# A macaron layer on one core: the latent masks and rows of constants move from the front of the program into the plan of its first half

## The chip, the cores and the metric

The kernel runs on one core of a Trainium2 chip. The metric is the device time of one execution in microseconds (us); lower is better. The core has five engines that run beside each other and wait for each other through semaphores: TensorE (PE, with its weight loads shown as PEld), VectorE (DVE), ScalarE (ACT), GpSimd (POOL) and SyncE (SP), which issues DMA transfers here. Each engine works through its own instructions strictly in the order in which the program lists them.

## The reference

The input x is 8 sequences of 512 tokens with 128 channels. The computation is two half-weighted blocks around a latent attention:

```python
x = x + 0.5 * ffn(layernorm(x))       # DEPTH = 2 layers of local attention and a gated MLP
x = x + attn(layernorm(x))            # causal attention, 16 heads of 8 channels
x = x + 0.5 * ffn(layernorm(x))       # the same weights again
```

A layer of `ffn` projects to q, k and v for 8 heads of 64 channels, normalises q and k, turns them by a rotary table, attends within windows of 64 tokens and the window before, and adds a product with `wo`; then a layernorm, a product with `w1`, `a * gelu(g)` and a product with `w2`. In `attn` the scores are masked so that a query sees only itself and the tokens before it, and the softmax runs over those.

## The kernel before, in words

Sequences b = 0 to 7 are cut into four blocks of 128 tokens. The program has three parts, one after the other: the first `ffn` with the beginning of the latent attention (`ffn("f0", last=False)`), the latent attention itself (`latent_attention`), and the second `ffn` (`ffn("f1", last=True)`).

In front of them stand loads and constants. Constants are made on POOL, in this order: the identity (by a helper in masks.py) and its 16-bit copy (L288), two band masks for the local attention (L294 to L306), and then what the latent attention needs: three masks `rows_of`, `causal` and `causal_t` of 128 x 512 in 16 bits, each by one memset (L317) and four `affine_select`, one for each quadrant of 32 partitions (L325), and `rows_sb`, two rows of constants (L332). `fill_rows` copies such a row by DMA into the tiles of the latent heads (L335); `maximum_products` and `sum_products` give the masks to TensorE (L1288, L1346 and their like).

Each `ffn` is written as steps, and a planner, `Plan`, puts them in order. A step has a kind, an engine, a cost in us that is written beside it, a rank, what it reads and writes, and the buffers that it takes. The rank is 100 times the number of the token block that the step belongs to, plus an entry of the table PLACE by kind. `Plan.run` deals out one step at a time: it looks at the steps in its window (for the `ffn` the 110 of lowest rank, `AHEAD`), works out from the written costs when each could start, takes the engine of the one that can start first, and on this engine the step of lowest rank that can start by then. It then traces the step, and binds each instruction behind the one before it on the same engine. So one more step on an engine changes the time at which the planner believes that engine to be free, and with it the order in which later steps are dealt, on the other engines too.

The constants in front are no steps: the planner begins with every engine free at time 0 and knows nothing of them. But they stand on POOL before POOL's first steps.

The steps that matter around the change, by lines:

- a layernorm: statistics on DVE (L484 to L486), logarithm and exponential on ACT (L467, L468) for the inverse root, a Newton step of four small instructions on POOL (L471 to L474), the result on DVE (L492)
- transposes of it on PE (L504), copied by ACT and DVE into `hT` (L528, L520); the first column of the lower half of `hT` is zeroed on POOL (L524)
- products with `wqkv` (L542); q and k are squared on ACT (L568) and multiplied by the rotary tables on DVE (L552, L555; the tables are made at L346 and L350), added on POOL (L576); the sums of squares on DVE (L600, L603), their root on ACT and its Newton step on POOL, and the scaling of k on POOL (L612)
- transposes of q and k (L504, copied at L642), scores (L665, L675), their maximum (L684, L685), the exponential on ACT (L692), the division by the sum on POOL (L700; its reciprocal on DVE, L716), transposes, the product with v (L758) and with `wo` (L782)
- products of weights for the latent attention, made once by `latent_weights` (L984 to L1004, rank of block 4 or 5 less 400)
- the beginning of the latent attention, at the end of the first plan (`latent_begins`): row fills by SP (kind "lo") and masked products of q and k for the maxima (kind "lm")

Of the kernel before, what the change touches and what calls it, by code (L numbers as in the profile page):

```python
# [10 lines left out]
BF16 = mybir.dt.bfloat16  # L11
AF = mybir.ActivationFunctionType
ALU = mybir.AluOpType
# [3 lines left out]
P = 128  # L17
MASKED = -1.0e30
# [15 lines left out]
}  # L34


# [152 lines left out]
def kernel(  # L189
# [21 lines left out]
    nc = tc.nc  # L211
# [80 lines left out]
    for first in (True, False):  # L292
        band = const.tile([P, P], BF16, name=f"band{int(first)}")
        nc.gpsimd.memset(band, 0.0)  # L294
        for half in (0, WIN):
            rows = band[half : half + WIN]
# [14 lines left out]
    def quadrant(g):  # L311
        return slice(32 * g, 32 * g + 32)

    masks = {}
    for name in ("rows_of", "causal", "causal_t"):
        masks[name] = const.tile([P, 4, P], BF16, name=name)
        nc.gpsimd.memset(masks[name], 0.0)  # L317
    for g in range(4):
        for name, pattern, sign, op, fill in (
            ("rows_of", [[-32, 4], [1, P]], -1, ALU.not_equal, 1.0),  # L320
            ("causal", [[32, 4], [-1, P]], 1, ALU.is_ge, MASKED),
            ("causal_t", [[-32, 4], [1, P]], -1, ALU.is_ge, MASKED),
        ):
            rows = masks[name][quadrant(g)]
            nc.gpsimd.affine_select(  # L325
                out=rows, in_=rows, pattern=pattern, compare_op=op, fill=fill, base=0,
                channel_multiplier=sign,
            )

    rows_sb = const.tile([4, 2, P], F32, name="rows_sb")  # L330
    for k in range(2):
        nc.gpsimd.memset(rows_sb[:, k], float(k))  # L332

    def fill_rows(dst, k):
        nc.sync.dma_start(  # L335
            out=dst[MD::32].rearrange("p j (n t) -> p (j n) t", t=P),
            in_=rows_sb[:, k].unsqueeze(1).to_broadcast([4, 4 * NB, P]),
        )
# [69 lines left out]
    def ffn(tagname, last):  # L408
        plan = Plan(tc, nc)

        def step(kind, engine, cost, at, *args, **kw):
            return plan.step(kind, engine, cost, 100 * at + PLACE[kind], *args, **kw)
# [514 lines left out]
        def first_loads():  # L927

            tables_u = Slot(r_u)
            size = 4 * NB * DH  # L930

            def rotary():
                return flat(tables_u.tile)[:, :size].rearrange(
                    "p (f n d) -> p f n d", f=4, n=NB
                )

            def scales():
                return flat(tables_u.tile)[:, size : size + 2 * L * DH].rearrange(
                    "p (s l d) -> p s l d", s=2, l=L
                )  # L940

            for t, scale in enumerate((q_scale, k_scale)):
                load_step(
                    0, lambda t=t, scale=scale: nc.sync.dma_start(
                        out=scales()[:, t].rearrange("p l d -> p (l d)"),
                        in_=scale.rearrange("l d -> (l d)").partition_broadcast(P),
                    ), [tables_u], [tables_u],
                )
            load_step(0, lambda: nc.sync.dma_start(out=rotary(), in_=rot), [tables_u], [tables_u])
            for l in range(L):  # L950
                for t in range(2):
                    step(
                        "tb", DVE, 1.2, 2 * l,
                        lambda l=l, t=t: rotary_table(l, t, rotary(), scales()),
                        [tables_u], [("tab", l, t)], [tables_u],
                    )
            load_step(0, lambda: nc.sync.dma_start(out=cols_sb, in_=cols), [("W", 0)])
            for what in load_layer(0):
                load_step(1, what, [("W", 0)])
            for b in range(1, B):  # L960
                load_step(NB * b, lambda b=b: load_tokens(b), [("X", b)])
            load_step(
                NB * 3, lambda: nc.sync.dma_start(out=wqkv_sb[1], in_=wqkv[1]), [("W", 1)]
            )
            for what in load_layer(1):
                load_step(NB * 4, what, [("W", 1)])
            latent_weights()

        def latent_weights():

            room, at = Slot(r_u), [0]

            def piece(rows, n):
                at[0] += n
                return lambda a=at[0]: flat(room.tile)[:rows, a - n : a]

            w = {}
            for name, src in (
                ("dq", w_dq), ("uq", w_uq), ("uq_t", w_uq_t), ("dkv", w_dkv), ("uk", w_uk),
                ("uv", w_uv), ("o_t", w_o_t),  # L980
            ):
                w[name] = piece(*src.shape)
                load_step(
                    4, lambda name=name, src=src: nc.sync.dma_start(out=w[name](), in_=src),  # L984
                    [("lw", name)], [room],
                )
            w["a"], w["keff"], w["veff"] = piece(QL, KVL), piece(KVL, C), piece(KVL, C)
            for n, name in enumerate(("full_q", "full_k", "full_v")):
                w[name] = lambda n=n: full[n]
            for lhsT, rhs, name in (  # L990
                ("uq", "uk", "a"), ("a", "dq", "keff"), ("uv", "o_t", "veff"),
                ("dq", "uq_t", "full_q"), ("dkv", "keff", "full_k"), ("dkv", "veff", "full_v"),
            ):
                ps = Slot(mm)

                def product(lhsT=lhsT, rhs=rhs, name=name, ps=ps):
                    rows, n = w[name]().shape
                    nc.tensor.matmul(
                        ps[:rows, :n], lhsT=w[lhsT](), rhs=w[rhs](), start=True, stop=True
                    )  # L1000

                def keep(name=name, ps=ps):
                    rows, n = w[name]().shape
                    nc.vector.tensor_copy(w[name](), ps[:rows, :n])  # L1004

                step("lw", PE, 0.3, 5, product, [("lw", lhsT), ("lw", rhs)], [ps], [ps, room], 0.1)
                step("lw", DVE, 0.25, 5, keep, [ps], [("lw", name)], [ps, room], 0.1)

        def latent_begins():
# [4 lines left out]
            for b in range(2):  # L1014
                q, kk, v = Slot(r_kT), Slot(r_V), Slot(r_V2)
                for name, t in (("q", q), ("k", kk), ("v", v)):
                    head_slots[name, b] = t
                    step(
                        "lz", POOL, 1.95, k, lambda t=t: nc.gpsimd.memset(t.tile, 0.0),
                        [], [t], [t], 0.0, [done[L - 1, B - 2 + b, NB - 1], done[L - 1, B - 1, 0]],  # L1020
                    )
                step("lo", SP, 0.55, k, lambda kk=kk: fill_rows(kk.tile, 1), [kk], [kk], [kk], 1.8)
                step(
                    "lz", POOL, 0.3, k,
                    lambda b=b: nc.gpsimd.memset(heads("v", b)[:, :, :, MD : MD + 1], 1.0),
                    [v], [v], [v],
                )
# [49 lines left out]
            for b, held in [(0, held) for held in MAXIMA] + [(1, held) for held in MAXIMA[:LEAD]]:  # L1077
                q, kk = head_slots["q", b], head_slots["k", b]
                m = maxima_of(b)
                for half in (0, 1):  # L1080
                    banks = [Slot(mm), Slot(mm)]
                    units = [
                        (2 * half + n, lambda n=n, banks=banks: banks[n].tile) for n in range(2)
                    ]
                    step(
                        "lm", PE, 1.3, k,
                        lambda b=b, held=held, units=units: by_turns(
                            [maximum_products(b, held, g, bank) for g, bank in units]
                        ),
                        [(q, "d"), (kk, "d")], banks, [q, kk] + banks, 0.1,  # L1090
                    )
                    for (g, bank), t in zip(units, banks):
                        step(
                            "lr", DVE, 0.63, k,
                            lambda m=m, held=held, g=g, bank=bank: maximum(m, held, g, bank()),
                            [t], [("max", b, g)], [t], 0.0,
                        )
# [521 lines left out]
```

## Time and profile before

| | us |
|---|---|
| median of 3 runs | 1879.91 |
| the runs | 1884.78, 1879.69, 1879.91 |
| profiled execution | 1883.39 |
| its span | 1881.6 |
| PE busy | 1757.7 |
| ACT busy | 1389.6 |
| DVE busy | 1373.7 |
| POOL busy | 990.1 |
| granted TensorE clock, mean | 0.98 of full |

Times in the profile are counted from the start of the span. A row of the timeline gives start, duration, engine, line of the kernel, operation, the tiles written and read, and in brackets how long the engine stood idle before it and what it waited for; rows that follow each other with the same form are merged with their count (x4). Durations overlap a little on one engine, because an instruction starts before the one ahead of it has quite ended. A row of the windows gives a stretch of time, its length, the busy time of each engine with the number of instructions, the granted clock, the busy share of the DMA engines and what they moved in GB/s. A suffix of _f on a tile's name means that it belongs to one of the two `ffn`.

### The profile page before, as it was taken

Reading aid. Unit: us, or ns where it says so; the run is one execution under the profiler, and the core shown is the slowest. Engines: PE = TensorE matmul, PEld = TensorE weight load, DVE = VectorE, ACT = ScalarE, POOL = GpSimd, SP = SyncE. Lnnn points to the kernel's source line nnn. Section 1 sums busy time; section 2 is a strip of 40 time slices with the busy share of each in tenths; the row PEclk is TensorE's granted clock in tenths of the full one; section 3 lists DMA queues with packets and bytes.
Section 4 is the critical chain, followed back from the end, with each engine's and each line's share of the span. In section 5 each row is a group of like instructions: output and inputs, shape, how many; then the busy total and the mean of one; then the engine's idle time right before and its main releaser. Section 6 shows DMA issues by size and latency. Waiting matters only on the chain.

```text
span 1881.6 us, 50927 instructions
## 1 busy us (share of the span) xinstructions
PE 1757.7 (93%) x19860; PEld 1179.0 (63%) x19860; DVE 1373.7 (73%) x2884; ACT 1389.6 (74%) x3911; POOL 990.1 (53%) x1685
## 2 busy tenths in 40 slices
PE   4899999999999989899999998989999999999998
PEld 2556666666666666467777764666666666666665
DVE  6888887777777867666766746878877777777764
ACT  2888878888888777236666666878888788778885
POOL 5776766666666665100000005867766666666651
PEclk9999999999999999769999999999999999999999
DMA  3111111111111111000000000111111111111110
GB/s 105 45 38 30 29 24 24 24 27 24 24 24 30 24 24 22 26 10 19 15 16 15 15 3 18 27 23 25 26 25 27 24 25 29 30 29 35 29 33 24
DMA packets 51968, 50.04 MB, mean 27 GB/s; under 512 B 22758, under 2 KB 34704, under 8 KB 51728
## 3 DMA queue, kind: packets, MB, share of 16 engines
q1 hardware_dynamic: 51584, 46.00, 10.5%
q8 instruction: 158, 2.59, 0.6%
q14 instruction: 82, 0.67, 0.1%
q10 hardware_dynamic: 144, 0.79, 0.1%
HBM read 6.30 MB, written 2.10 MB: 4 GB/s over the span
## 4 chain that ended last, share of the span: by engine, by line
PE 56%; DVE 18%; ACT 14%; POOL 6%; issue 4%; DMA 1%; SPq 1%; ACTq 0%; DVEq 0%; POOLq 0%
PE mm_f L542 9%; PE mm_f L504 8%; ACT pr_f L692 5%; PE mm_f L849 5%; PE st L1355 4%; PE mm_f L891 4%; PE mm_f L758 4%; PE mm_f L782 3%; PE lo L1372 3%; PE sc L1297 3%; DVE c_f L552 3%; DVE s_f L555 3%; PE sc_f L675 3%; ACT sq_f L568 2%; PE mm_f L1297 2%
## 5 line engine op out<-in xcount | busy, mean ns | idle before, releaser
L692 ACT ACTIVATE pr_f<-sc_f,nm_f,q_f 128x128 f32<-128x128 f32 x1024 | 460.3, 475 | 5.5 <-DVE nm_f L685 5.1
L542 PE MATMUL mm_f<-wqkv,hT_f 128*128 128x512 f32 x768 | 391.3, 613 | 30.4 <-DVE s_f L555 14.0
L576 POOL TENSOR_TENSOR qk_f<-c_f,s_f 128x512 f32<-128x512 f32 x256 | 325.0, 1274 | 115.1 <-DVE s_f L555 112.8
L700 POOL TENSOR_TENSOR pr_f<-pr_f,rso_f 128x512 f32<-128x512 f32 x256 | 266.0, 1040 | 220.8 <-DVE rso_f L716 180.7
L552 DVE TENSOR_TENSOR c_f<-mm_f,tab 128x512 f32<-128x512 f32 x256 | 175.3, 685 | 79.0 <-PE mm_f L542 34.6
L692 ACT ACTIVATION_READ_ACCUMULATOR pr_f<-sc_f,nm_f,q_f 128x1 f32 x1024 | 226.4, 221 | 0.0
L568 ACT ACTIVATE sq_f<-mm_f 128x512 f32<-128x512 f32 x256 | 153.1, 608 | 87.4 <-DVE s_f L555 61.4
L1366 ACT ACTIVATE pl<-st 128x512 f32<-128x512 f32 x280 | 152.8, 597 | 73.9 <-PE st L1355 59.8
L849 PE MATMUL mm_f<-fT_f,w 128*128 128x512 f32 (+1 forms) x384 | 190.5, 611 | 8.9 <-ACT ge_f L855 7.0
L504 PEld LDWEIGHTS mm_f<-ident,qk_f 128*128 128x128 f32 x1024 | 114.7, 141 | 128.9 <-POOL qk_f L612 52.1
L504 PE MATMUL mm_f<-ident,qk_f 128*128 128x128 f32 x1024 | 160.0, 280 | 31.8 <-POOL qk_f L612 12.8
L542 PEld LDWEIGHTS mm_f<-wqkv,hT_f 128*128 128x128 f32 x768 | 125.0, 192 | 99.1 <-issue 42.0
L684 DVE TENSOR_REDUCE nm_f<-sc_f 128x8 f32<-128x1024 f32 x128 | 155.3, 1214 | 42.6 <-PE sc_f L675 42.5
L758 PEld LDWEIGHTS mm_f<-pT_f,V_f 128*64 128x64 f32 (+1 forms) x4096 | 147.4, 136 | 60.2 <-issue 13.1
L758 PE MATMUL mm_f<-pT_f,V_f 128*64 128x64 f32 (+1 forms) x4096 | 179.8, 230 | 0.7 <-ACT pT_f L738 0.7
L555 DVE TENSOR_TENSOR s_f<-mm_f,tab 128x512 f32<-128x512 f32 x256 | 174.0, 680 | 0.0
L1387 POOL TENSOR_TENSOR X<-X,lon 128x128 f32<-128x128 f32 x26 | 11.9, 456 | 306.2 <-DVE lon L1381 306.2
L504 PE MATMUL mm_f<-ident,pr_f 128*128 128x128 f32 x1024 | 155.9, 280 | 11.5 <-DVE u_f L880 3.0
L504 PEld LDWEIGHTS mm_f<-ident,pr_f 128*128 128x128 f32 x1024 | 116.3, 142 | 74.1 <-POOL pr_f L700 33.0
L600 DVE TENSOR_REDUCE rn_f<-sq_f 128x16 f32<-128x1024 f32 x128 | 153.7, 1201 | 7.5 <-ACT sq_f L568 7.5
L782 PEld LDWEIGHTS mm_f<-wo,oT_f 128*128 128x128 f32 x1024 | 127.7, 191 | 43.0 <-ACT oT_f L771 18.1
L782 PE MATMUL mm_f<-wo,oT_f 128*128 128x128 f32 x1024 | 140.7, 280 | 3.2 <-ACT oT_f L771 2.9
(166 smaller groups left out, 3865.2 us busy)
## 6 DMA issues: line engine op xcount, KB each, us to landing
V_f<-V_f SPq DMA_DIRECT2D x224, 128.0 KB
hs_f<-Y SPq DMA_DIRECT2D x32, 112.0 KB
X<-in_x_dram SPq DMA_DIRECT2D x8, 256.0 KB
out_dram<-hs_f SPq DMA_DIRECT2D x8, 256.0 KB
Y<-fl SPq DMA_DIRECT2D x32, 32.0 KB
kT_f<-fl SPq DMA_DIRECT2D x32, 32.0 KB
V_f<-fl SPq DMA_DIRECT2D x32, 32.0 KB
wqkv<-in_wqkv_dram ACTq DMA_DIRECT2D x1, 768.0 KB
```

Source lines behind the costliest of these rows:

```text
L504: nc.tensor.transpose(dst[:, i * P : (i + 1) * P], src(i), ident)
L542: nc.tensor.matmul(ps.tile, lhsT=hT[:, i * P : (i + 1) * P], rhs=wqkv_sb[l][:, at * INNER : (at + 1) * INNER], start=True, stop=True,)
L552: nc.vector.tensor_mul(c1.tile, psv, tabs[l][:, 2 * s, i].unsqueeze(1).to_broadcast([P, H, DH]))
L555: nc.vector.tensor_mul(s1.tile.rearrange("p h (t d) -> p h t d", t=2), psv.rearrange("p h (t d) -> p h t d", t=2)[:, :, ::-1], tabs[l][:, ...
L568: lambda s=s, ps=ps: nc.scalar.activation(sq[:, s], ps.tile, AF.Square),
L576: lambda s=s, c1=c1, s1=s1: nc.gpsimd.tensor_add(qk[:, s].rearrange("p (h d) -> p h d", d=DH), c1.tile, s1.tile),
L684: nc.vector.tensor_reduce(nm.tile, sv, AX.X, ALU.max, negate=True)
L692: nc.scalar.activation(pr[:, h], sv[:, h % 2, h // 2], AF.Exp, bias=nm[:, h % 2, h // 2 : h // 2 + 1], scale=q8[:, h : h + 1], accum_out=s ...
L700: nc.gpsimd.tensor_mul(pr[:, heads], pr[:, heads], inv[:, heads].unsqueeze(2).to_broadcast([P, H // 2, P]),)
L758: nc.tensor.matmul(o[r * DH : (r + 1) * DH, u * P + w * WIN : u * P + (w + 1) * WIN], lhsT=(V2, V)[w][keys, i, h * DH : (h + 1) * DH], rhs ...
L782: nc.tensor.matmul(pw[:, :C], lhsT=oT[:, pr], rhs=wo_sb[l][:, pr], start=(pr == 0), stop=(pr == INNER // P - 1),)
L849: nc.tensor.matmul(ps[: hsz[c], :], lhsT=w1_sb[l][:, at + c * P : at + c * P + hsz[c]], rhs=fT.tile, start=True, stop=True,)
```

## The change

The masks and the rows of constants get their tiles in front as before, but the instructions that fill them become 17 steps of kind "lb" on POOL in the first plan: three memsets, twelve selects and two small memsets. Each has a written cost of 0.65 us and a rank of 500, that of token block 5. The four selects of a mask now follow its memset; before, the selects went around the three masks. The row fills of `latent_begins` and the products for its maxima name "masks" among what they read, so that the planner puts them behind the 17 steps. The rows of the second row fill ("l4") stay as they are.

```diff
-    "lw": -400, "tb": -450, "fi": 990, "fo": 1230,
+    "lw": -400, "lb": 0, "tb": -450, "fi": 990, "fo": 1230,
...
-    masks = {}
-    for name in ("rows_of", "causal", "causal_t"):
-        masks[name] = const.tile([P, 4, P], BF16, name=name)
-        nc.gpsimd.memset(masks[name], 0.0)
-    for g in range(4):
-        for name, pattern, sign, op, fill in (
...
-            rows = masks[name][quadrant(g)]
-            nc.gpsimd.affine_select(
-                out=rows, in_=rows, pattern=pattern, compare_op=op, fill=fill, base=0,
-                channel_multiplier=sign,
-            )
+    MASKS = (
+        ("rows_of", [[-32, 4], [1, P]], -1, ALU.not_equal, 1.0),
+        ("causal", [[32, 4], [-1, P]], 1, ALU.is_ge, MASKED),
+        ("causal_t", [[-32, 4], [1, P]], -1, ALU.is_ge, MASKED),
+    )
+    masks = {name: const.tile([P, 4, P], BF16, name=name) for name, *_ in MASKS}
 
     rows_sb = const.tile([4, 2, P], F32, name="rows_sb")
-    for k in range(2):
-        nc.gpsimd.memset(rows_sb[:, k], float(k))
+
+    def mask_parts():
+
+        for name, pattern, sign, op, fill in MASKS:
+            yield lambda name=name: nc.gpsimd.memset(masks[name], 0.0)
+            for g in range(4):
+                rows = masks[name][quadrant(g)]
+                yield lambda rows=rows, pattern=pattern, sign=sign, op=op, fill=fill: (
+                    nc.gpsimd.affine_select(
...
+        for k in range(2):
+            yield lambda k=k: nc.gpsimd.memset(rows_sb[:, k], float(k))
...
             latent_weights()
+            for what in mask_parts():
+                step("lb", POOL, 0.65, 5, what, [], ["masks"])
...
-                step("lo", SP, 0.55, k, lambda kk=kk: fill_rows(kk.tile, 1), [kk], [kk], [kk], 1.8)
+                step(
+                    "lo", SP, 0.55, k, lambda kk=kk: fill_rows(kk.tile, 1), [kk, "masks"], [kk],
+                    [kk], 1.8,
+                )
...
-                        [(q, "d"), (kk, "d")], banks, [q, kk] + banks, 0.1,
+                        [(q, "d"), (kk, "d"), "masks"], banks, [q, kk] + banks, 0.1,
```

More of the change, by code (lines that the diff above doesn't have):

```diff
@@ L312, in quadrant @@
         return slice(32 * g, 32 * g + 32)
-    masks = {}
-    for name in ("rows_of", "causal", "causal_t"):
-        masks[name] = const.tile([P, 4, P], BF16, name=name)
-        nc.gpsimd.memset(masks[name], 0.0)
-    for g in range(4):
-        for name, pattern, sign, op, fill in (
[L320 to L323, printed above, removed]
-            rows = masks[name][quadrant(g)]
-            nc.gpsimd.affine_select(
-                out=rows, in_=rows, pattern=pattern, compare_op=op, fill=fill, base=0,
-                channel_multiplier=sign,
-            )
-    rows_sb = const.tile([4, 2, P], F32, name="rows_sb")
-    for k in range(2):
-        nc.gpsimd.memset(rows_sb[:, k], float(k))
+    MASKS = (
[4 more added lines that the diff above has]
+    masks = {name: const.tile([P, 4, P], BF16, name=name) for name, *_ in MASKS}
+    rows_sb = const.tile([4, 2, P], F32, name="rows_sb")
+    def mask_parts():
[5 more added lines that the diff above has]
+                    nc.gpsimd.affine_select(
+                        out=rows, in_=rows, pattern=pattern, compare_op=op, fill=fill, base=0,
+                        channel_multiplier=sign,
+                    )
+                )
+        for k in range(2):
+            yield lambda k=k: nc.gpsimd.memset(rows_sb[:, k], float(k))
     def fill_rows(dst, k):
@@ L1021, in latent_begins @@
                     )
-                step("lo", SP, 0.55, k, lambda kk=kk: fill_rows(kk.tile, 1), [kk], [kk], [kk], 1.8)
+                step(
+                    "lo", SP, 0.55, k, lambda kk=kk: fill_rows(kk.tile, 1), [kk, "masks"], [kk],
+                    [kk], 1.8,
+                )
                 step(
```

## The prediction

> **What bounds the kernel now.** First the page's lines by engine and by slice: TensorE is busy for 93% of the span, GpSimd (POOL) for 53%. The chain of waits gives POOL 6% of the span, and TensorE is almost empty in the first slice. So I read the timeline of the first 20 us, which is where the removed instructions stand.
>
> ```profile
> span 1881.6 us, 50927 instructions
> ## 1 busy us (share of the span) xinstructions
> PE 1757.7 (93%) x19860; PEld 1179.0 (63%) x19860; DVE 1373.7 (73%) x2884; ACT 1389.6 (74%) x3911; POOL 990.1 (53%) x1685
> ```
>
> ```profile
> 4.00 0.65 POOL L301 TENSOR_SCALAR_AFFINE_SELECT band<-band 64x128 bf16<-64x128 bf16 x2
> 4.71 0.53 POOL L317 MEMSET rows_of<- 128x512 bf16 x1
> ...
> 6.22 0.63 POOL L325 TENSOR_SCALAR_AFFINE_SELECT rows_of<-rows_of 32x512 bf16<-32x512 bf16 x1
> ...
> 8.33 0.21 ACT L468 ACTIVATE ns_f<-ns_f 128x4 f32<-128x4 f32 x1
> ...
> 13.67 0.34 POOL L332 MEMSET rows_sb<- 4x128 f32 x2
> 14.06 0.14 POOL L524 MEMSET hT_f<- 64x1 f32 x2
> 14.28 0.20 POOL L471 TENSOR_TENSOR nt_f<-ns_f 128x4 f32<-128x4 f32 x1
> ...
> 15.12 0.20 POOL L474 TENSOR_TENSOR ns_f<-ns_f,nt_f 128x4 f32<-128x4 f32 x1
> 15.36 1.12 DVE L492 TENSOR_SCALAR Y<-X,mv_f,ns_f 128x128 f32<-128x128 f32 x4 [7.30 <-POOL ns_f L474]
> ...
> 15.76 1.24 PE L504 MATMUL mm_f<-ident,Y 128*128 128x128 f32 x4 [15.76 <-DVE Y L492]
> ```
>
> The first column is the start, the second the duration. The first layernorm has left ScalarE at 8.54 (8.33 + 0.21), but its Newton step on POOL starts at 14.28, behind the masks; VectorE waits 7.30 us for it, and TensorE starts at 15.76. The chain runs through L317 and L325 here.
>
> Then the stage into which the change moves the masks: POOL's timeline and the windows (busy time of PE, PEld, DVE, ACT, POOL).
>
> ```profile
> 73.35 1.26 POOL L576 TENSOR_TENSOR qk_f<-c_f,s_f 128x512 f32<-128x512 f32 x1
> 78.71 1.27 POOL L576 TENSOR_TENSOR qk_f<-c_f,s_f 128x512 f32<-128x512 f32 x1 [4.10 <-DVE s_f L555]
> 79.94 1.04 POOL L700 TENSOR_TENSOR pr_f<-pr_f,rso_f 128x512 f32<-128x512 f32 x1
> 82.29 1.27 POOL L576 TENSOR_TENSOR qk_f<-c_f,s_f 128x512 f32<-128x512 f32 x1 [1.30 <-DVE s_f L555]
> ```
>
> ```profile
> 79.00:112.00 33.00, 30.42 (x338) 19.80 (x337) 26.96 (x54) 26.56 (x88) 26.45 (x49) 1.00 0.18 42
> 112.00:150.00 38.00, 34.18 (x334) 22.22 (x335) 29.52 (x68) 31.78 (x98) 25.70 (x40) 1.00 0.12 25
> 150.00:250.00 100.00, 98.45 (x1040) 67.12 (x1039) 85.78 (x191) 84.18 (x255) 68.75 (x120) 1.00 0.13 31
> ```
>
> POOL has one hole of 4.10 us, then is busy for 80% of 79 to 112 (26.45 of 33). TensorE stands idle for 8% there (2.58 us), 10% in the next stretch, and 1.6% in the one after.
>
> **Removed in front.** Three memsets, twelve selects and two small memsets hold POOL from 4.71 to 14.01: 9.30 us (memsets 0.47 apart, selects 0.60 apart). Without them POOL ends its constants at 4.65 and does the two hT_f memsets, and the Newton step can start 0.07 after ScalarE (27.40 + 0.21 to 27.68 in the second norm): at 8.61 instead of 14.28, that is **5.67 us** earlier, not 9.30; what is late next is ScalarE's root. The order of each engine stays the same up to the masks' new place, so the whole ramp moves together unless a load holds it. The loads bear it, by the trace's records of DMA packets: the rotary table's (4096 bytes) have all landed at 10.04, and its first reader (L346, 16.39 now) would want it at 10.72; the first wqkv has landed before 6; and X's second batch, landed by 14.82, is wanted at 25.24 - 5.67 = 19.6. I take -5.67.
>
> **Added in the plan.** The same 17 instructions, now in 17 steps; none issues a DMA. In the order of the changed program they stand on POOL from place 92 to 117 of 1690, between the L576 that is at 73.35 now and the stage at some 95 us. The first seven (two memsets, five selects: 2 x 0.47 + 5 x 0.60 = 3.94) come before the L700 of 79.94 and so fall into the 4.10 us hole: nothing. If that cover were gone they would cost up to their 3.94. The other ten (9.30 - 3.94 = 5.36) stand between the steps that run from 79.94 to 95.04. Queued behind them are the divide of the probabilities (L700), the k side's rotary sum (L576) and the Newton step of the q and k norms; TensorE waits for these to transpose. From below: POOL's waits up to 95 (1.30 + 0.46 + 0.51 = 2.27) and 1.33 more by 97.65 take them in, and the chain between 79 and 112 passes through PE, DVE and ACT and no POOL row: 0 us. From above: all 5.36 arrive at TensorE. I take what is left when the waits before 95.04 are used up, 5.36 - 2.27 = **+3.1 us**, because from 98.6 to 111.5 POOL has no wait in which to catch up.
>
> **Reordered.** The planner sees POOL taken and deals the other steps differently: POOL, ScalarE and VectorE come back to the old order at what is now 246.9, 249.9 and 250.4 us. The work is the same; only TensorE's idle time can change. Bounds: it can give back no more than the 2.58 us idle of 79 to 112 where the masks lie, and it can keep TensorE idle at the 10% of 112 to 150 through the 100 us after it as well (rival 2). I put the rest at zero: work of the same size in a similar mix.
>
> **New waits.** The row fills (SP, first at 733.6) and the maxima's products (L1288, first at 771.5) wait for masks that are finished some 600 us before: nothing on SP or PE. The latent half and the second plan keep their order.
>
> **Clock.** Granted clock is 0.84 in 28 to 60, and the trace has half-clock stretches of 6.83 and 3.41 us there; at half clock the weight loads of L542 are 0.85 apart (19.42, 20.28), later 0.43 (22.77, 23.20). If one such 3.41 us stretch comes or goes when the ramp moves, that is 1.7 us either way; I put zero. [...]
>
> **Sum.** -5.67 + 3.1 + 0 = -2.6 us. The profiled execution took 1883.39 (span 1881.6 and 1.8 around it), so 1880.8 by its own measure; it stands 3.5 above the median of the runs, 1879.91, to which I apply the same difference: **1877.3 us**, or -0.14%. A change of 0.3% (5.6 us) is about what a measurement of this kernel can tell from none; its own runs lie between 1879.69 and 1884.78.
>
> **Rivals.**
> 1. *All hidden.* POOL's waits swallow the ten instructions and the reordering gives back some of TensorE's 2.58 us: -5.67 to -8.25, 1871.7 to 1874.2, say 1873. For it: no POOL row on the chain of that stage. Against: POOL's unbroken 13 us from 98.6.
> 2. *Ragged until the orders meet (slower).* The late k side leaves scores and probabilities late, and TensorE idles in 150 to 250 as in 112 to 150: 10.1% - 1.55% = 8.5 us more, on top of all 5.36: -5.67 + 13.9 = +8.2, 1888. It decides once the added idle time exceeds 5.67 us. For it: the order is changed for 170 us, and TensorE has only 1.55 us of idle time in the last 100 to lose. Against: rings of two to five buffers, and ACT and DVE at 84 and 86%, so not full.
> 3. *The front does not pay.* Something else holds the ramp (a load, the clock), the saving is gone and the 3.1 us stay: 1883. Against: the landings above.
>
> **How the numbers follow.** Forecast 0.50 (its own range, from all hidden to 5.36 us: 1874.2 to 1879.6); rival 1 0.27; rival 2 0.17; rival 3 0.06. Rival 1 lies beyond -0.3% (below 1874.3): faster 0.27. Rival 2 lies mostly above 1885.6: slower 0.16, its remaining 0.01 with the forecast and rival 3 within 0.3%: 0.57. The range leaves a little on each side: from 1871.5 (rival 1 with the idle time given back) to 1886 (most of the way to rival 2).
>
> **What would show it.** In the changed profile: the first Newton step at 8.6 and TensorE's first matmul at 10.1; selects of about 0.63 us in a row in POOL's former hole, at some 69 to 73; the latent half's first products (771.5 now) earlier by the net change, 2.6, since nothing after 250 us is reordered. If they are earlier by 5.7 or more, rival 1; if later, rival 2. I am wrong if TensorE's idle time between the hole and the meeting of the orders grows by more than 5.36 us or not at all.

## The result and the profile after

The changed kernel takes 1877.92 us in the median of 21 runs, the kernel before 1881.18 in 21 runs beside them: 3.3 us less. The ratio is 0.9981 with a 95% interval of 0.9973 to 0.9990, so between 1.9 and 5.1 us of gain, and within the 0.3% that the prediction gave as its bound. It had said -2.6 us. The profiled execution took 1879.79 us.

The page of the changed kernel gives the span and the busy times, with hardly a difference from before: the work is the same.

```profile
span 1878.0 us, 50920 instructions
## 1 busy us (share of the span) xinstructions
PE 1759.4 (94%) x19860; PEld 1178.8 (63%) x19860; DVE 1373.3 (73%) x2884; ACT 1384.8 (74%) x3911; POOL 988.8 (53%) x1685
```

The timeline of its start shows the front (lines after the change are four to nine higher in number: L475 was L471, L496 was L492, L508 was L504, L330 was L325).

```profile
3.98 0.62 POOL L301 TENSOR_SCALAR_AFFINE_SELECT band<-band 64x128 bf16<-64x128 bf16 x2
4.56 0.13 POOL L528 MEMSET hT_f<- 64x1 f32 x2
...
8.23 0.20 ACT L472 ACTIVATE ns_f<-ns_f 128x4 f32<-128x4 f32 x1
...
8.59 0.20 POOL L475 TENSOR_TENSOR nt_f<-ns_f 128x4 f32<-128x4 f32 x1 [3.90 <-ACT ns_f L472]
...
9.66 1.11 DVE L496 TENSOR_SCALAR Y<-X,mv_f,ns_f 128x128 f32<-128x128 f32 x4 [1.70 <-POOL ns_f L478]
...
10.06 1.25 PE L508 MATMUL mm_f<-ident,Y 128*128 128x128 f32 x4 [10.06 <-DVE Y L496]
```

POOL now waits 3.90 us for ScalarE, where before ScalarE's result lay waiting for POOL, and TensorE begins at 10.06, 5.7 us earlier than before. POOL's timeline in the former hole and behind it:

```profile
67.35 1.27 POOL L580 TENSOR_TENSOR qk_f<-c_f,s_f 128x512 f32<-128x512 f32 x1
68.57 0.53 POOL L326 MEMSET rows_of<- 128x512 bf16 x1
69.17 2.66 POOL L330 TENSOR_SCALAR_AFFINE_SELECT rows_of<-rows_of 32x512 bf16<-32x512 bf16 x4
71.89 0.52 POOL L326 MEMSET causal<- 128x512 bf16 x1
72.48 0.63 POOL L330 TENSOR_SCALAR_AFFINE_SELECT causal<-causal 32x512 bf16<-32x512 bf16 x1
73.47 1.04 POOL L704 TENSOR_TENSOR pr_f<-pr_f,rso_f 128x512 f32<-128x512 f32 x1 [0.36 <-DVE rso_f L720]
74.58 1.30 POOL L330 TENSOR_SCALAR_AFFINE_SELECT causal<-causal 32x512 bf16<-32x512 bf16 x2
...
81.09 2.66 POOL L330 TENSOR_SCALAR_AFFINE_SELECT causal_t<-causal_t 32x512 bf16<-32x512 bf16 x4
83.83 1.04 POOL L704 TENSOR_TENSOR pr_f<-pr_f,rso_f 128x512 f32<-128x512 f32 x1
```

The first seven stand in the hole, which ends with a wait of 0.36 us, and the other ten lie between the steps behind it. The windows of the changed kernel over the stretch that answers to 79 to 250 of before:

```profile
73.00:107.00 34.00, 31.64 (x342) 21.18 (x343) 26.00 (x55) 26.34 (x87) 30.37 (x52) 0.95 0.15 33
107.00:145.00 38.00, 34.84 (x375) 23.07 (x372) 31.18 (x72) 31.43 (x100) 27.37 (x49) 1.00 0.14 33
145.00:246.00 101.00, 97.48 (x999) 65.44 (x998) 82.00 (x191) 83.47 (x255) 68.56 (x120) 1.00 0.13 29
```

POOL is now busy for 30.37 of 34 us where the masks are. TensorE's idle time is not worse there (2.36 us, against 2.58 in 33 us before); over all three rows it is 9.04 us in 173, against 7.95 in the 171 of the three rows before. But in the first row the granted clock is 0.95: the trace has a stretch of 3.41 us at half clock from 74.1.

**How the traces are compared from here on.** One kernel's times scatter by some 2 us from run to run, as much as the effect. So the lead is also read from the traces: the start of each ScalarE instruction less the start of the same instruction in one and the same trace of the kernel before (its second one, run e7_before_again), and of these the median over ten microseconds. Negative is earlier; the column "end" compares the spans. Where the order on the engines is that of before, the same place in the order is the same instruction; where it differs (79 to 250 in the changed kernel), no lead is given. The last column is the ratio of the measured times, with its 95% interval.

| trace | 70 to 80 | 300 to 310 | 720 to 730 | end | ratio of times (95%) |
|---|---|---|---|---|---|
| before, first trace | +0.2 | 0.0 | +1.1 | +0.8 | |
| after | -5.8 | -4.7 | -4.8 | -2.8 | 0.9981 (0.9973 to 0.9990) |
| e8_after_again | -5.5 | -3.2 | -1.5 | -1.7 | 0.9979 (0.9970 to 0.9988) |
| e1_late | -5.8 | -7.3 | -7.3 | -1.4 | 1.0008 (0.9999 to 1.0017) |
| e2_reorder | +2.9 | +2.2 | +1.0 | -1.2 | 1.0003 (0.9995 to 1.0012) |
| e3_zero | -6.0 | -0.4 | -1.4 | -1.5 | 1.0000 (0.9991 to 1.0009) |
| e4_double | +8.0 | +6.4 | +5.3 | +4.3 | 1.0040 (1.0027 to 1.0052) |
| e5_spread | -6.1 | -5.4 | -5.4 | -5.2 | 0.9972 (0.9962 to 0.9981) |
| e6_block20 | -5.7 | +2.3 | +2.1 | +1.6 | 1.0010 (1.0001 to 1.0018) |
| e9_hole7 | -5.7 | -5.6 | -6.1 | -7.9 | 0.9980 (0.9970 to 0.9990) |
| e10_spread65 | -6.0 | -5.7 | -7.2 | -4.9 | 0.9968 (0.9958 to 0.9979) |

A step in a row that happens at the masks belongs to them. Steps elsewhere of one or two microseconds happen between executions of one and the same program too: the two traces of before move against each other by +1.1 and back, at half-clock stretches that only one of them has (681 in the first, 1115 in the second). The kernels e1_late, e3_zero, e4_double, e5_spread and e9_hole7 have the order of before on all engines but for the masks (and one neighbouring pair on POOL in e1_late).

### The profile page after: what moved, and what is told of

Its sections match the earlier page's. It is cut to its first block, busy times and chain, and to the rows that moved or that the text cites. A ratio compares the mean times of both kernels' runs of the same rounds, so it can differ in the third digit from the quotient of the medians.

```text
span 1878.0 us, 50920 instructions
## 1 busy us (share of the span) xinstructions
PE 1759.4 (94%) x19860; PEld 1178.8 (63%) x19860; DVE 1373.3 (73%) x2884; ACT 1384.8 (74%) x3911; POOL 988.8 (53%) x1685
## 4 chain that ended last, share of the span: by engine, by line
PE 57%; DVE 18%; ACT 14%; POOL 5%; issue 4%; DMA 1%; SPq 1%; DVEq 0%; ACTq 0%; POOLq 0%
PE mm_f L546 9%; PE mm_f L508 8%; ACT pr_f L696 5%; PE mm_f L853 5%; PE mm_f L895 4%; PE mm_f L762 4%; PE st L1364 4%; PE mm_f L786 4%; PE lo L1381 3%; PE sc L1306 3%; DVE c_f L556 3%; DVE s_f L559 3%; PE sc_f L679 3%; ACT sq_f L572 3%; DVE nm_f L688 2%
## 5 line engine op out<-in xcount | busy, mean ns | idle before, releaser
L580 POOL TENSOR_TENSOR qk_f<-c_f,s_f 128x512 f32<-128x512 f32 x256 | 324.8, 1273 | 111.7 <-DVE s_f L559 104.6
L704 POOL TENSOR_TENSOR pr_f<-pr_f,rso_f 128x512 f32<-128x512 f32 x256 | 265.8, 1039 | 204.5 <-DVE rso_f L720 174.2
L508 PEld LDWEIGHTS mm_f<-ident,qk_f 128*128 128x128 f32 x1024 | 114.7, 141 | 125.4 <-POOL qk_f L616 51.6
L508 PE MATMUL mm_f<-ident,qk_f 128*128 128x128 f32 x1024 | 160.3, 281 | 29.1 <-POOL qk_f L616 11.6
L508 PE MATMUL mm_f<-ident,pr_f 128*128 128x128 f32 x1024 | 155.4, 279 | 13.0 <-ACT V_f L588 2.9
L508 PEld LDWEIGHTS mm_f<-ident,pr_f 128*128 128x128 f32 x1024 | 116.5, 142 | 78.7 <-POOL pr_f L704 32.4
```

The lines of the kernel that those rows point to most:

```text
L508: nc.tensor.transpose(dst[:, i * P : (i + 1) * P], src(i), ident)
L580: lambda s=s, c1=c1, s1=s1: nc.gpsimd.tensor_add(qk[:, s].rearrange("p (h d) -> p h d", d=DH), c1.tile, s1.tile),
L704: nc.gpsimd.tensor_mul(pr[:, heads], pr[:, heads], inv[:, heads].unsqueeze(2).to_broadcast([P, H // 2, P]),)
```

## The experiments

### The front alone: e1_late

```diff
+            late = [done[L - 1, B - 2, NB - 1], done[L - 1, B - 1, 0]]
+            for what in mask_parts():
+                step("lb", POOL, 0.0, k - 11, what, [], ["masks"], behind=late)
             for b in range(2):
                 q, kk, v = Slot(r_kT), Slot(r_V), Slot(r_V2)
```

(in `latent_begins`, in place of the steps behind `latent_weights`)

> The masks leave the front and are made just before their first readers, in 17 steps of written cost 0, so that no other step is dealt in another order. This is the front's saving alone. My theory (the sum of the prediction): -5.7 us against the kernel before, and every instruction from the first norm to the end of the first half starts 5.7 us earlier. Rival 3 (something else holds the ramp): between 0 and -3.

In time it is no faster than before: ratio 1.0008, so the -5.7 us expected are missed. The trace says where the saving went. The lead is 5.8 us at 70, and 7.3 at 720: the front's saving is there and stays through the whole first half. Then it falls from -7.3 to +0.3 within twenty microseconds. POOL's timeline there:

```profile
718.94 0.20 POOL L478 TENSOR_TENSOR ns_f<-ns_f,nt_f 128x4 f32<-128x4 f32 x1
719.07 0.53 POOL L326 MEMSET rows_of<- 128x512 bf16 x1
719.68 2.66 POOL L330 TENSOR_SCALAR_AFFINE_SELECT rows_of<-rows_of 32x512 bf16<-32x512 bf16 x4
...
729.19 0.34 POOL L336 MEMSET rows_sb<- 4x128 f32 x2
729.48 1.79 POOL L1026 MEMSET kT_f<- 128x2048 f32 x1
731.35 1.04 POOL L704 TENSOR_TENSOR pr_f<-pr_f,rso_f 128x512 f32<-128x512 f32 x1
```

The row of masks stands before the division of the last probabilities (L704), and the waits of the same stretch show TensorE waiting for it:

```profile
PE mm_f L508 <- POOL pr_f L704: 6.0, 1, 6.0
```

So rival 3 of the prediction falls (the front does pay, and the lead does not shrink on the ramp), and the place that I had chosen for the masks was a bad one. POOL is busy for only half of that slice of the page of before (5 tenths in 706 to 753), and yet its row of ten microseconds costs 7.6.

Not all of that is the wait. The trace has 6.83 us of half clock from 731.3. By the starts of TensorE's own instructions against the second trace of before, the lead is 7.7 us before the wait, 1.9 at its end (732.45), and turned into a lag of 0.3 at 738.5, where the stretch has ended: some 5.8 us go in the wait and 2.2 behind it at half clock.

### The order alone: e2_reorder

```diff
+    for part_ in mask_parts():
+        part_()
...
             for what in mask_parts():
-                step("lb", POOL, 0.65, 5, what, [], ["masks"])
+                step("lb", POOL, 0.65, 5, lambda: None, [], ["masks"])
```

> The masks stay in front as before; the plan gets 17 steps of cost 0.65 that issue nothing, so all engines have the changed kernel's order and POOL has no extra work after the front. This is the reordering alone. My theory: 0, within 1.5 us. Rival (the order is what costs the changed kernel its part of the saving): +1.3 us, the 4.4 us that the changed profile's middle is early against 5.7. Rival (the order gives idle time back): -2 us or below, with the masks then costing more than 3 us.

The ratio is 1.0003: no difference that can be measured, as expected. The lead goes from +2.9 at 70 to +2.2 at 300, so the order by itself gives back 0.7 us, about as much as two traces of one program differ. The +2.9 comes from the ramp and has two parts: the masks stand one behind the other in front here, which takes POOL 0.8 us longer (first Newton step at 15.06 against 14.28), and this execution has 13.65 us of half clock from 32.1, where before has 6.83.

### Inserted without reordering: e3_zero

```diff
-                step("lb", POOL, 0.65, 5, what, [], ["masks"])
+                step("lb", POOL, 0.0, 5, what, [], ["masks"])
```

> The masks are steps of rank 500 with written cost 0: they stand in a row at POOL's places 92 to 108, in the 4.1 us hole, and all other steps keep the order of before. Front saved, masks inserted, nothing reordered. My theory: the 5.4 us that do not fit into the hole arrive at TensorE less what POOL's later waits take in: -5.7 + 3.1 = -2.6 us, at worst -0.3. Rival 1 (all hidden): -5.7.

The ratio is 1.0000, so the -2.6 us expected are missed; the -0.3 given as the worst fits. The lead falls from 6.0 us to 0.4: the masks cost 5.6 us here, about all that does not fit into the hole and not the 3.1 that I had taken. POOL's timeline, and TensorE's beside it:

```profile
68.41 0.53 POOL L326 MEMSET rows_of<- 128x512 bf16 x1
...
78.35 0.34 POOL L336 MEMSET rows_sb<- 4x128 f32 x2
78.77 1.26 POOL L580 TENSOR_TENSOR qk_f<-c_f,s_f 128x512 f32<-128x512 f32 x1
79.99 1.04 POOL L704 TENSOR_TENSOR pr_f<-pr_f,rso_f 128x512 f32<-128x512 f32 x1
```

```profile
75.06 1.15 PE L762 MATMUL mm_f<-pT_f,V_f 128*64 128x64 f32 x32
81.08 1.12 PE L508 MATMUL mm_f<-ident,pr_f 128*128 128x128 f32 x4 [4.87 <-POOL pr_f L704]
81.99 1.92 PE L546 MATMUL mm_f<-wqkv,hT_f 128*128 128x512 f32 x2
```

TensorE waits 4.87 us for the division behind the masks. After the wait its clock is halved: the windows, cut at 79, show a granted clock of 0.98 and then of 0.50.

```profile
73.00:79.00 6.00, 3.22 (x40) 1.84 (x38) 2.64 (x6) 3.05 (x11) 5.49 (x11) 0.98 0.20 44
79.00:85.00 6.00, 3.92 (x13) 2.89 (x14) 3.36 (x6) 3.52 (x13) 5.58 (x10) 0.50 0.00 0
```

The half-clock stretch is 6.83 us long from 78.8. It begins within the wait: TensorE works until 76.22, 2.6 us ahead of it.

By TensorE's own starts against the second trace of before, its lead is 6.0 us until 70.4, 5.5 behind the hole (72.79), 0.6 at the end of the wait (81.08), and gone at 86.03, where the stretch has ended. So the wait for POOL costs 4.9 us, the hole 0.5 and the half rate some 0.65.

### The front doubled: e4_double

The three memsets and twelve selects stand twice in front of the plan of before.

```diff
+    for name in ("rows_of", "causal", "causal_t"):
+        nc.gpsimd.memset(masks[name], 0.0)
+    for g in range(4):
+        for name, pattern, sign, op, fill in (
...
+            nc.gpsimd.affine_select(
```

> The three memsets and twelve selects stand in front twice, 9.0 us more on POOL ahead of the first norm's Newton step. If the front lies on the chain with nothing beside it: +9.0 us, and the first matmul at 24.8 instead of 15.8. If the ramp has slack behind it or the clock takes a part: less, 5 to 7.

The ratio is 1.0040 (1.0027 to 1.0052), +5.1 to +9.8 us. The first matmul comes at +9.0, and at 70 the lag is 8.0: the front lies on the chain, and the ramp makes up 1 us of the 9. The time fits both of the expectations.

### One piece a block: e5_spread

```diff
-            for what in mask_parts():
-                step("lb", POOL, 0.65, 5, what, [], ["masks"])
+            for n, what in enumerate(mask_parts()):
+                step("lb", POOL, 0.0, 8 + n, what, [], ["masks"])
```

> The 17 steps have written cost 0 and ranks 800, 900, and so on to 2400, one for each token block from the eighth on, so that single selects of 0.6 us stand between POOL's other instructions over some 200 us and nothing else is reordered. Theory after the first four runs: the row of masks in one place is what costs (5.4 us beyond the hole all arrive at TensorE when nothing is reordered), and single pieces go into POOL's short waits where TensorE is busy for 98%: -5 to -5.7 us against the kernel before. Rival (POOL's results are wanted at once everywhere, in a stage where it is busy for 70%): each piece arrives at TensorE with that share, 9.3 x 0.7 = 6.5, so +0.8.

The ratio is 0.9972 (0.9962 to 0.9981): 3.6 to 7.2 us faster than before. The lead falls from 6.1 to 5.4 only, and there is no half-clock stretch between 31 and 754. The same pieces, then, 0.7 us net in place of 5.6. One of them in POOL's timeline:

```profile
109.41 1.04 POOL L704 TENSOR_TENSOR pr_f<-pr_f,rso_f 128x512 f32<-128x512 f32 x1
110.40 0.62 POOL L330 TENSOR_SCALAR_AFFINE_SELECT rows_of<-rows_of 32x512 bf16<-32x512 bf16 x1
111.00 1.25 POOL L580 TENSOR_TENSOR qk_f<-c_f,s_f 128x512 f32<-128x512 f32 x1
```

This one has no wait on either side, so it pushes POOL by 0.6 us, and TensorE feels it. Here are VectorE and TensorE beside it, and then the same two instructions in the second trace of before:

```profile
110.76 1.52 DVE L490 TENSOR_SCALAR rs_f<-mv_f 128x4 f32<-128x4 f32 x1
113.49 0.70 PE L546 MATMUL mm_f<-wqkv,hT_f 128*128 128x512 f32 x1 [2.11 <-ACT V_f L588]
```

```profile
116.83 0.94 DVE L486 TENSOR_SCALAR rs_f<-mv_f 128x4 f32<-128x4 f32 x1
118.97 0.70 PE L542 MATMUL mm_f<-wqkv,hT_f 128*128 128x512 f32 x1 [1.53 <-ACT V_f L584]
```

In both, VectorE's instruction ends 0.02 to 0.03 us after the rotary sum on POOL (L580, L576) beside it; with the sum pushed by 0.6 us it takes 1.52 us in place of 0.94, 0.58 longer, and TensorE, behind ScalarE, waits 0.58 us longer too. At 127 another 0.5 us of the lead go, and 0.8 come back at 135. The 0.7 is what is left of such losses and gains, and not a sign that each piece is free.

### A row further back: e6_block20

```diff
-                step("lb", POOL, 0.65, 5, what, [], ["masks"])
+                step("lb", POOL, 0.65, 20, what, [], ["masks"])
```

> The changed kernel with rank 2000 in place of 500: the planner deals the 17 steps of 0.65 together some 160 us later, where TensorE stands idle for under 2%, and reorders a short stretch around them. Theory (the planner's reordering hides a row of masks that it is told of): -4 to -5.7 us. Rival (in the changed kernel the order only happened to fall well): the row of 9.3 us costs as without reordering, 0 to -1.

The ratio is 1.0010 (1.0001 to 1.0018), slightly slower than before. The lead of 5.7 us holds until 200 and is a lag of 2.3 at 300: the row costs 8.0 us although the planner was told of it; the -4 to -5.7 us expected are missed. The windows around it:

```profile
145.00:236.00 91.00, 88.86 (x926) 59.78 (x924) 77.20 (x168) 74.98 (x224) 63.47 (x110) 1.00 0.13 31
236.00:262.00 26.00, 20.86 (x200) 13.33 (x200) 17.97 (x38) 16.85 (x56) 20.89 (x38) 0.87 0.12 26
```

TensorE is idle for 5.14 of 26 us, and the trace has 6.83 us of half clock from 252.2, whose share of the 8.0 us cannot be told apart here. So the planner's reordering does not hide such a row as a rule. In the changed kernel it happened to.

### Two programs again: e7_before_again, e8_after_again

> The kernel before once more, for a second trace of it: the clock's stretches of half rate and the waits for transfers then show what differs between two executions of one program. Theory: 0 in time, and a difference of several us between the traces' shifts over the span, at the half-clock stretches. Rival (executions agree, and the differences seen between the kernels' traces after 250 us belong to the change): shifts under 0.5 us everywhere.

Ratio 1.0004 (0.9995 to 1.0013). The two traces agree within 0.7 us up to 680; later they are apart by +1.1, then -0.3, at most +2.5, at half-clock stretches. The rival falls: such steps after 250 us are no part of the change.

> The changed kernel once more: theory -3.4 us as before, first matmul at 10.1, and TensorE's idle time between 73 and 107 below 3 us again, with or without a half-clock stretch there. Rival (the half-clock stretch at 74 comes from the change): it is there again at the same place.

Ratio 0.9979 (0.9970 to 0.9988), as before. The half-clock stretch of 3.41 us is there again, but at 88.6 instead of 74.1, and TensorE's idle time between 73 and 107 is 3.19 us, more than I had said. The masks cost 2.3 us in this trace (5.5 to 3.2) and 1.1 in the other (5.8 to 4.7). Neither trace of before has such a stretch between 57 and 681. It is not bound to the place, so the rival falls as it was worded, but both executions of the changed kernel have one where the masks are.

```profile
73.00:107.00 34.00, 30.81 (x338) 20.58 (x338) 25.76 (x52) 25.42 (x83) 29.83 (x48) 0.95 0.15 33
```

The two traces are of one program, with the stretch at different places, and so they show what it costs. Before 73, the first is 0.3 us ahead on TensorE and on POOL. In its stretch at 74.1 TensorE falls 1.6 us back, but POOL stays 0.3 ahead up to 93, and by 88.4 TensorE has made up all but some 0.4, because in the second trace TensorE waits 0.85 and 0.77 us for POOL (at 86.78 and 88.21). In the second trace's stretch at 88.6 TensorE loses 1.5 us, POOL falls 0.9 further back behind it, and the first trace stays 1.3 to 1.4 ahead up to 300. So the first stretch cost at most some 0.4 us in the end and the second some 1.1, about the difference of the two prices, 1.1 and 2.3.

### The hole by itself: e9_hole7

```diff
-            for what in mask_parts():
-                step("lb", POOL, 0.65, 5, what, [], ["masks"])
+            for n, what in enumerate(mask_parts()):
+                step("lb", POOL, 0.0, 5 if n < 7 else 8 + n, what, [], ["masks"])
```

> The first seven steps (two memsets, five selects) have rank 500, the other ten ranks from 1500 on, one a block; all with written cost 0, so nothing else is reordered. It asks whether POOL's 4.1 us hole takes the seven for nothing, as the prediction has it. If so: -5 to -5.5 us, like the pieces spread out, and no change of the lead of 5.8 us between 65 and 80 us. Since four selects of one mask in a row stand 0.67 apart in the changed trace and not 0.60, the seven take some 4.5 us: the lead may fall by 0.4. Rival (POOL is wanted again before the hole ends): the lead falls by 1 or more and the time is at most 4 us shorter.

The lead falls from 5.7 at 70 to 5.2 from 90 to 130: 0.5 us. POOL's timeline shows why it is not nothing: the row now reaches to the next step without a wait.

```profile
68.67 0.53 POOL L326 MEMSET rows_of<- 128x512 bf16 x1
69.27 2.66 POOL L330 TENSOR_SCALAR_AFFINE_SELECT rows_of<-rows_of 32x512 bf16<-32x512 bf16 x4
71.98 0.52 POOL L326 MEMSET causal<- 128x512 bf16 x1
72.58 0.63 POOL L330 TENSOR_SCALAR_AFFINE_SELECT causal<-causal 32x512 bf16<-32x512 bf16 x1
73.28 1.28 POOL L580 TENSOR_TENSOR qk_f<-c_f,s_f 128x512 f32<-128x512 f32 x1
```

Seven take 4.6 us (68.67 to 73.28) in a hole of 4.1. The time, 0.9980 (0.9970 to 0.9990), is 1.9 to 5.6 us shorter, which does not tell the two expectations apart; the lead does.

### Spread, with the planner told: e10_spread65

```diff
-            for what in mask_parts():
-                step("lb", POOL, 0.65, 5, what, [], ["masks"])
+            for n, what in enumerate(mask_parts()):
+                step("lb", POOL, 0.65, 8 + n, what, [], ["masks"])
```

> The steps spread over blocks 8 to 24 as in e5_spread, but with the changed kernel's written cost of 0.65, so that the planner reorders a stretch around the first ones. Theory: what counts is that the masks lie apart, so -5 us as there. Rival (telling the planner of them costs or gains by how the order falls): more than 1.5 us away from -5.

Ratio 0.9968 (0.9958 to 0.9979): 3.9 to 7.9 us faster than before, 1874.11 in the median against 1880.07. It and e5_spread, whose interval overlaps, are the fastest of all; the intervals of both also touch that of the changed kernel, so that they beat it is likely and not shown by the times alone. The lead after the masks, 5.7 and 5.4 us against 4.7 and 3.2, says the same. It too has a half-clock stretch of 3.41 us, from 113.0.

## Why the prediction was right, and where not

**Removed in front, -5.67: right.** The first Newton step came at 8.59 (forecast 8.61) and the first matmul at 10.06 (10.1). The lead stands at 5.5 to 6.1 us up to the masks in every kernel without the front, and e1_late carries it to 720. The loads did not hold the ramp.

**Added, the first seven in the hole, nothing: nearly right.** They cost 0.5 us (e9_hole7). The size was off because I took 0.60 us for a select, measured where the selects went around three tiles; one behind the other on the same tile they start 0.67 apart (2.66 for four), and the whole row takes 10.3 us (68.41 to 78.69 in e3_zero) instead of 9.30.

**Added, the other ten, +3.1: the term that was mis-sized.** Without reordering they cost 5.1 (5.6 in e3_zero less 0.5 for the hole's seven), near the upper bound of 5.36 and not what POOL's waits leave over. The working counted waits that come after the masks; TensorE had by then already stood waiting for the division queued behind them, and a later wait of POOL gives that back to nobody. The trace of e3_zero shows both: POOL does come back, from 0.2 us behind the second trace of before at 78.77 to 1.6 ahead at 83.21, as the working had it, but TensorE has lost all but some 0.5 us of its lead by then. As single pieces the same work costs 0.7 net (e5_spread). In these runs the price goes by how long the row is that the next wanted instruction has to stand behind, and not by the sum of the work.

**Reordered, 0: wrong as a term.** By itself the order is worth -0.7 us, within what two traces differ. But together with the masks it saves most of their price: 1.1 and 2.3 us in the two traces of the changed kernel against 5.6 in the old order. What the planner changes can be seen on POOL: in e3_zero all 17 stand in one row of 10.3 us, while in the changed kernel the ten behind the hole stand in groups between the steps that are wanted, the longest of them 4.0 us (79.80 to 83.83). In e6_block20 the planner leaves a row of 6.7 us (234.23 to 240.97). That the shorter rows make the difference is argued, not shown: the order on the other engines changes with them. I had added insertion and reordering as if each kept its own price. The errors of the two terms offset each other: +3.1 + 0 was forecast, +1.1 to +2.3 is what the traces show. The ratios 0.9981 and 0.9979 are some 3.6 and 4.0 us of gain, which leaves 1.6 to 2.0 of a front of 5.6. So the total came out near partly by luck; the front's term and the sign rest on a working that held.

**How well the prices are known.** The kernel e1_late has no masks between the front and 719, and from 70 to 300 it gains 1.5 us on the second trace of before. Measured against it, every price is 1.5 us higher: 7.1 in e3_zero, 2.6 and 3.8 in the changed kernel, 2.2 in e5_spread, 1.8 in e10_spread65. Their order stays, but no single price is known to better than some 1.5 us, and by this measure the sum of the two terms, +3.1, lies within what the changed kernel shows.

**Clock, 0 give or take 1.7: it held.** Both traces of the changed kernel have one more stretch of 3.41 us at half clock at the masks. Set beside each other (e8_after_again) they show that the first cost at most some 0.4 us in the end and the second some 1.1. That the masks have a part in it is my estimate: the seven in the hole lengthen one idle time of TensorE from 1.5 to 2.0 us (70.94 to 72.95 in the first trace), and 1.1 us behind it the first trace's stretch begins. But the same 2.0 us stand at 71.23 in the second trace and at 71.05 in e9_hole7, with no half clock behind them; what makes the difference is not shown.

**The test by the latent half.** Its first masked product came at 766.3 instead of 771.5: 5.2 us earlier, not 2.6. Against the second trace of before (769.9) it is 3.6. Most of the difference of 1.6 is the half-clock stretch at 681 in the first (1.1): a test by one trace at one place was too coarse for what it should tell. The other sign named there, TensorE's idle time, did what it had to: it grew by 1.1 us over the stretch (9.04 less 7.95), more than nothing and less than 5.36.

**The rivals.** All hidden (rival 1) did not happen in the changed kernel, but nearly does in e5_spread and e10_spread65. Ragged and slower (rival 2) did not happen there either, but, by little, in e6_block20 with the same code and another rank. Which of them a place gives could not be read from the row of busy shares: the price depended on what was queued behind the masks.

## What to carry to other kernels

The work that moved off the start-up chain gave back the whole time by which the next result came earlier, and here that could be read to a tenth of a microsecond from the timeline. What it cost at its new place was not its length less the engine's idle time: ask which instruction stands behind the whole row, and who waits for that one. A row of ten microseconds cost 5 to 8 in three places of an engine that is busy for 53% of the span, with the half clock behind it, and cut into single pieces 0.6 us long, one a block, 0.7 to 2.2; a planner told of the row hid most of it in one place and none of it in another.

## What the runs showed that was not expected

- Selects on the same tile one behind the other start 0.67 us apart, selects that go around three tiles 0.59 to 0.70, on average 0.62: the grouping by mask, with a memset between the groups, makes the row 1.0 us longer.
- The half-clock stretches that do not run into the end of the span are 3.41 us long or multiples of it (6.83, 10.24, 13.65, 40.96). The twelve traces have 8 of them between 60 and 700 us, and in the 3.41 us ahead of each TensorE is busy for 0.87 to 1.72 us (1.41 ahead of that at 74.1 in the changed kernel's first trace, where the rest is the idle time of 2.0 us). What sets such a stretch off is not shown: the same 2.0 us have none behind them in e9_hole7 and e8_after_again.
- In e1_late, e4_double and e9_hole7 some 1.1 us are gained between 130 and 150, in e5_spread 0.8, in e3_zero and e6_block20 nothing. It goes with one short instruction of VectorE, that of L490 (L486 before, L500 in e4_double), here in e1_late and in the second trace of before:

```profile
133.48 0.31 DVE L490 TENSOR_SCALAR rs_f<-mv_f 128x4 f32<-128x4 f32 x1
```

```profile
139.64 1.14 DVE L486 TENSOR_SCALAR rs_f<-mv_f 128x4 f32<-128x4 f32 x1
```

  It takes 0.17 to 0.31 us at this place in the four that gain, where it starts just before POOL's rotary sum, and 0.88 to 1.17 in e3_zero, e6_block20 and both traces of before, where it starts 0.1 to 0.4 us behind the start of that sum and ends with it. Over the whole of the two traces of before it takes 0.17 us in the median where no POOL instruction of over 0.9 us runs beside it (70 times), and 0.76 where one does (30 times, 22 of them ending 0.02 to 0.03 us after it). So a few tenths of a microsecond by which the two engines are shifted can cost or save TensorE about one; that this is the cause here is read from the traces, not tested by a run of its own.
